# Two feed-forward layers with eight of 64 experts around a gated mixing layer, on one core: row transfers by index from POOL, and one product's halves issued together

## The chip, the cores and the metric

The kernel runs on one core of a Trainium2 chip. A core has five engines, each with its own queue of instructions in program order: PE (TensorE, matrix products and transposes), DVE (VectorE), ACT (ScalarE), POOL (GpSimd) and SP (SyncE, which here only issues transfers). Engines wait for each other through semaphores. The core's 16 DMA engines move data between the device memory and the on-chip memory. PE writes to PSUM, a small memory that DVE and ACT read.

The metric is the device time of one launch in microseconds (us). Lower is better.

## What is computed

The input `u` has 8 sequences of 512 tokens with 128 features, in float32. With x = u:

```python
x = x + 0.5 * ffn(layernorm(x))
x = x + mix(layernorm(x))
x = x + 0.5 * ffn(layernorm(x))          # the same weights again

def ffn(x):                              # 64 experts, hidden size 64, the best 8 per token
    shared = silu(x @ Ws_up) @ Ws_down
    aff = x @ centroids.T                # "logits"
    idx = top_k(aff + expert_biases, 8)
    w = sigmoid(aff[idx]);  w = w / (sum(w) + 1e-8)
    h = silu(einsum('td,edf->etf', x, W_up))
    y = einsum('etf,efd->etd', h, W_down)
    return shared + einsum('etd,te->td', y, cw)    # cw: w at the chosen experts, else 0

def mix(u):
    xf = u @ WB.T,  but the first token as it is
    xb = u @ WBf.T, but the last token as it is
    gamma = sigmoid(xf @ w1.T + xb @ w2.T + b)
    return gamma * (xf + xb) + (1 - gamma) * u
```

All 64 experts are computed for every token; those that were not chosen have weight 0.

## The kernel before

**Items.** The work is 16 items: `items` lists the two ffn layers, and within each the 8 sequences. An item is one sequence in one layer, held as four tiles of 128 tokens (`NT` = 4) in `xs[s]`, 128 partitions by 4 by 128. In the second layer `mix(s)` runs before the ffn of the sequence. Two experts make a pair (2 x 64 hidden = 128), so an item has 32 pairs (`NP`).

**The main loop** (L460 to L484) runs over n, 16 x 32 pairs and 25 more. It writes each engine's order out by hand, since `manual_schedule` keeps program order. Step n does this:

- `up(n)`: PE multiplies the pair's `W_up` with the item's transposed tokens `ut` into `ph` (128x512, L410). ACT writes silu of it to `h` (L412). Four `ph` buffers exist.
- `scale(n - 22)`: DVE multiplies `h` of 22 steps ago with the routing weights `cw` (L418). `load_cw` (L293) brings these from device memory on SP, four pairs at a time, broadcast over 64 partitions.
- `down(n - 25)`: PE multiplies the scaled `h` of 25 steps ago with `W_down` and accumulates into `y` (L428). After pair 31, ACT writes half of `y` to `yt` (L452).
- `finish(i)`, two steps after an item's last `down`: PE transposes `yt` four times into `po` (L396), DVE adds it to `xs[s]` (L397), and in the second layer SP issues one store of the sequence (L399).
- one step of `prep(i + 1)`, the preparation of the next item.

A float32 product is two instructions on PE in the profile (hence x1024 for 512 products).

**Preparation.** `prep(i)` is a generator: each `yield` ends its part of one step. It starts at pair 1 of the item before (for item 1: at pair 14 of item 0, `FIRST`). In order:

- in the second layer all of `mix(s)`: `stats`, `normed`, `turned`, the products `pfb`, the gate, the update of `xs[s]`
- `stats` (L179): DVE takes mean and variance of the four tiles (L184, L186), POOL makes `rstd` with an add and a power (L188, L189)
- `normed` (L192): four DVE instructions write `u` (L195)
- two yields later, `turned` (L205): four PE transposes into one PSUM buffer (L209), and ACT copies it to `ut` (L318)
- a step later the shared-and-logits product `sl` (L327): for each half of the tokens (256), one product with `wsl`, whose 128 columns are `Ws_up` and the transposed centroids. Half 0 has them in one order, half 1 in the other. DVE copies the logits' 64 rows to `lg` (L335), and ACT writes silu of the other 64 to `hsh` (L336)
- a step later PE transposes `lg` into `pa` (L342); then DVE and ACT choose the experts and make the weights; PE transposes these, and SP stores them to device memory (`cw_t`, L387, L388)

The loop that issues the two halves of `sl`, as it stands:

```python
for k in range(2):
    nc.tensor.matmul(sl[:, k, :], lhsT=wsl[:, k, :, :]..., rhs=ut[:, k * H : (k + 1) * H], ...)
    at, other = slice(k * F, (k + 1) * F), slice((1 - k) * F, (2 - k) * F)
    nc.vector.tensor_copy(lg[other, :], sl[other, k, :])
    nc.scalar.activation(hsh[at, :], sl[at, k, :], AF.Silu)
```

`sl` is one PSUM tile, `[P, 2, H]`.

**Transfers.** All are issued by SP, in program order. Ahead of the loop come sequence 0 (`load_x(0)`, L98), centroids, `Ws_up`, `W_up` in four parts, sequence 1 and half of `W_down`. `load_rest` (L137) is called at pair 14 of item 0, after the first four `load_cw`, and before the first step of `prep(1)`. It issues the rest: `Ws_down`, the other half of `W_down`, sequences 2 to 7, and the mixing layer's weights.

**Pools.** The PSUM pool `ps_m` has two buffers, shared by all transposes, `sl`, `pfb` and `po`. Each sequence has its own `xs` tile.

Of the kernel before, what the change touches and what calls it, by code (L numbers as in the profile page):

```python
# [8 lines left out]
F32 = mybir.dt.float32  # L9
AF = mybir.ActivationFunctionType  # L10
ALU = mybir.AluOpType
AX = mybir.AxisListType

P = 128
EPS_LN = 1e-5
# [11 lines left out]
def macaron_kernel(  # L27
# [34 lines left out]
    nc = tc.nc  # L62
    B, T, D = x.shape
    E, _, F = w_up.shape
    NT = T // P
# [3 lines left out]
    H = T // 2  # L69
    NH = NT // 2  # L70
    assert D == P and 2 * F == P and E == F and NT == 4 and NP % GROUP == 0

    const = ctx.enter_context(tc.tile_pool(name="const", bufs=1))
# [9 lines left out]
    ps_m = ctx.enter_context(tc.tile_pool(name="ps_m", bufs=2, space=bass.MemoryType.PSUM))  # L83
# [10 lines left out]
    warm = const.tile([P, 1], F32, name="warm")  # L94
    nc.scalar.activation(warm, ident[:, 0:1], AF.Silu)

    def load_x(s):
        nc.sync.dma_start(out=xs[s], in_=x[s].rearrange("(n p) d -> p n d", p=P))  # L98

    wup = const.tile([P, E, F], F32, name="wup")  # L100
    wdn = const.tile([P, NP, D], F32, name="wdn")
# [19 lines left out]
            in_=w_down[e0:e1].rearrange("(q two) f d -> (two f) q d", two=2),  # L121
        )

    load_x(0)
    nc.sync.dma_start(out=cent, in_=centroids)
    for k in range(2):
        nc.sync.dma_start(out=wsl[:, k, k, :], in_=ws_up)
# [9 lines left out]
    def load_rest():  # L137

        for k in range(2):
            nc.sync.dma_start(out=wsdn[k * F : (k + 1) * F, :], in_=ws_down)  # L140
        load_down(E // 2, E)
        for s in range(2, B):
            load_x(s)
        nc.sync.dma_start(out=wb_sb, in_=wb)
        nc.sync.dma_start(out=wbf_sb, in_=wbf)
        nc.sync.dma_start(out=w12[:, 0, :], in_=w1[0].partition_broadcast(P))
        nc.sync.dma_start(out=w12[:, 1, :], in_=w2[0].partition_broadcast(P))
        with nc.allow_non_contiguous_dma(reason="two columns, once"):
            nc.sync.dma_start(out=w12c[:, 0:1], in_=w1.rearrange("o d -> d o"))
            nc.sync.dma_start(out=w12c[:, 1:2], in_=w2.rearrange("o d -> d o"))  # L150
        nc.sync.dma_start(out=b_bc, in_=b.partition_broadcast(P))
# [24 lines left out]
        nc.scalar.mul(half_b, b_bc, 0.5)  # L176


    def stats(src, name):  # L179

        st = small.tile([P, NT, nc.vector.BN_STATS_DIM], F32, tag="st", name=f"st_{name}")
        mv = small.tile([P, NT, nc.vector.BN_AGGR_DIM], F32, tag="mv", name=f"mv_{name}")
        for j in range(NT):
            nc.vector.bn_stats(st[:, j, :], src[:, j, :])  # L184
        for j in range(NT):
            nc.vector.bn_aggr(mv[:, j, :], st[:, j, :])  # L186
        rstd = small.tile([P, NT], F32, tag="rstd", name=f"rstd_{name}")
        nc.gpsimd.tensor_scalar(rstd, mv[:, :, 1], EPS_LN, None, ALU.add)  # L188
        nc.gpsimd.tensor_tensor(rstd, rstd, minus_half, ALU.pow)  # L189
        return mv, rstd  # L190

    def normed(src, mv, rstd, width, name):  # L192
# [9 lines left out]
            )  # L202
        return u

    def turned(src, name):  # L205

        ps = ps_m.tile([P, 512], F32, tag="m", name=f"ps_{name}")
        for j in range(NT):
            nc.tensor.transpose(ps[:, j * P : (j + 1) * P], src[:, j, :D], ident)  # L209
        return ps  # L210

    def mix(s):
        xt = xs[s]
        mv, rstd = stats(xt, f"mix{s}")
        yield
        u = normed(xt, mv, rstd, D1, f"mix{s}")

        for k, j in ((0, 0), (1, NT - 1)):
            ew = norm.tile([P, D], F32, tag="ew", name=f"ew{s}_{k}")
            nc.vector.tensor_tensor(ew, u[:, j, :D], w12[:, k, :], ALU.mult)  # L220
            nc.vector.tensor_reduce(u[:, j, D:D1], ew, AX.X, ALU.add)
        yield
        yield
        ps = turned(u, f"mixt{s}")


        ut = norm.tile([P, T + 1], F32, tag="mixt", name=f"mixt{s}")
        nc.gpsimd.memset(ut[:, 0:1], 0.0)
        nc.gpsimd.memset(ut[:, T : T + 1], 0.0)
        nc.scalar.copy(ut[:, 1:T], ps[:, 1:T])  # L230
        yield
        yield
        gam = small.tile([P, NT], F32, tag="gam", name=f"gam{s}")
        halves = []
        for half in range(NT // 2):
            pfb = ps_m.tile([P, 2, D1], F32, tag="m", name=f"pfb{s}_{half}")
            halves.append(pfb)
            for k in range(2):
                j = 2 * half + k
                nc.tensor.matmul(  # L240
                    pfb[:, k, :],
                    lhsT=ut[:, j * P : (j + 1) * P],
                    rhs=mix_b,
                    start=True,
                    stop=False,
                )
                nc.tensor.matmul(  # L247
                    pfb[:, k, :],
                    lhsT=ut[:, j * P + 1 : (j + 1) * P + 1],
                    rhs=mix_bf,  # L250
                    start=False,
                    stop=True,
                )

            k, j, at = ((0, 0, 0), (1, NT - 1, P - 1))[half]
            nc.vector.scalar_tensor_tensor(  # L256
                pfb[:, k, :], u[:, j, :], ident[:, at : at + 1], pfb[:, k, :], ALU.mult, ALU.add
            )
            nc.scalar.activation(  # L259
                gam[:, 2 * half : 2 * half + 2],  # L260
                pfb[:, :, D],
                AF.Tanh,
                bias=half_b,
                scale=0.5,
            )
            yield
        sg = small.tile([P, NT], F32, tag="sg", name=f"sg{s}")
        nc.vector.tensor_scalar(sg, gam, 0.5, 0.5, ALU.mult, ALU.add)
        rest = small.tile([P, NT], F32, tag="rest", name=f"rest{s}")
        nc.vector.tensor_scalar(rest, gam, -0.5, 0.5, ALU.mult, ALU.add)  # L270
        for j in range(NT):
            nc.vector.scalar_tensor_tensor(
                xt[:, j, :],
                halves[j // 2][:, j % 2, :D],
                sg[:, j : j + 1],
                xt[:, j, :],
                ALU.mult,
                ALU.add,
            )
        yield  # L280
        for j in range(NT):
            nc.vector.scalar_tensor_tensor(
                xt[:, j, :], u[:, j, :D], rest[:, j : j + 1], xt[:, j, :], ALU.mult, ALU.add
            )
        yield
# [20 lines left out]
    def prep(i):  # L306

        layer, s = items[i]
        if layer == 1:
            yield from mix(s)  # L310
        mv, rstd = stats(xs[s], f"f{i}")
        yield
        u = normed(xs[s], mv, rstd, D, f"f{i}")
        yield
        yield
        ps = turned(u, f"ft{i}")
        ut = norm.tile([P, T], F32, tag="ut", name=f"ut{i}")
        nc.scalar.copy(ut, ps)  # L318
        uts[i] = ut
        yield  # L320

# [4 lines left out]
        for k in range(2):  # L326
            nc.tensor.matmul(  # L327
                sl[:, k, :],
                lhsT=wsl[:, k, :, :].rearrange("d a f -> d (a f)"),
                rhs=ut[:, k * H : (k + 1) * H],  # L330
                start=True,
                stop=True,
            )
            at, other = slice(k * F, (k + 1) * F), slice((1 - k) * F, (2 - k) * F)
            nc.vector.tensor_copy(lg[other, :], sl[other, k, :])  # L335
            nc.scalar.activation(hsh[at, :], sl[at, k, :], AF.Silu)  # L336
# [54 lines left out]
    def finish(i, yt):  # L391

        layer, s = items[i]
        po = ps_m.tile([P, NT, D], F32, tag="m", name=f"po{i}")
        for j in range(NT):
            nc.tensor.transpose(po[:, j, :], yt[:, j * P : (j + 1) * P], ident)  # L396
        nc.vector.tensor_tensor(xs[s], po, xs[s], ALU.add)  # L397
        if layer == 1:
            nc.sync.dma_start(out=out[s].rearrange("(n p) d -> p n d", p=P), in_=xs[s])  # L399


    hs = {}
# [21 lines left out]
    def down(n):  # L424
        i, pair = divmod(n, NP)
        if pair == 0 and i not in ys:
            ys[i] = ps_y.tile([P, T], F32, tag="y", name=f"y{i}")
        nc.tensor.matmul(  # L428
            ys[i],
            lhsT=wdn[:, pair, :],  # L430
            rhs=hs.pop(n),
            start=pair == 0 and i % 2 == 0,
            stop=pair == NP - 1,
        )


        if i % 2 == 0 and pair in SHARED:
            if i + 1 not in ys:
                ys[i + 1] = ps_y.tile([P, T], F32, tag="y", name=f"y{i + 1}")
            k = SHARED.index(pair)  # L440
            for at, item in sorted(((k, i), (1 - k, i + 1))):
                rows = slice(at * F, (at + 1) * F)
                nc.tensor.matmul(  # L443
                    ys[item][:, at * H : (at + 1) * H],
                    lhsT=wsdn[rows, :],
                    rhs=shared[item][rows, :],
                    start=item > i and k == 0,
                    stop=False,
                )
        if pair == NP - 1:  # L450
            yt = norm.tile([P, T], F32, tag="yt", name=f"yt{i}")
            nc.scalar.mul(yt, ys.pop(i), 0.5)  # L452
            later[n + 2] = lambda: finish(i, yt)

    total = len(items) * NP
# [71 lines left out]
```

## Time and profile before

| | |
|---|---|
| device time, median of 3 runs | 985.75 us (985.08 to 985.78) |
| the profiled execution: device time | 985.12 us |
| its span, first to last instruction | 983.0 us |
| granted TensorE clock, mean | 0.999 |
| `ph`, L410: 1024 instructions | 523.3 us busy, mean 595 ns |
| `y`, L428: 1024 instructions | 518.8 us busy, mean 592 ns |
| DVE `h` by `cw`, L418: 512 instructions | 322.1 us busy, mean 681 ns |
| ACT silu, L412: 512 instructions | 303.4 us busy, mean 597 ns |
| POOL `rstd`, L188 and L189 for the ffn: 16 each | 8.5 and 16.6 us busy |
| moved by SP's queue | 145.18 MB, 69.9% of the time of 16 DMA engines |

How to read the profile: a row of the groups gives line, engine, operation, output and inputs by their names in the program, shapes and count; behind the bar the busy time and the mean of one instruction in ns; behind the second bar how long the engine stood idle just before these instructions, and what ended most of that. A row of the timeline has start, duration, engine, line, operation, output and inputs, and in brackets the idle time before it with its releaser. PEld is the weight load of PE, which lies beside the products. SPq is SP's queue: its rows are the issuing of transfers, not the data on the way. Durations of PE overlap, since products are pipelined; the distance between two starts tells more.

### The profile page before, as it was taken

What the parts mean: (1) busy time and instruction counts of PE and PEld (TensorE: products, weight loads), DVE (VectorE), ACT (ScalarE), POOL (GpSimd) and SP (SyncE); (2) the same over time, 40 slices, a digit from 0 to 9 for tenths busy, and PEclk for the clock granted to TensorE, in tenths of its full rate; (3) what the DMA queues carried; (4) which work ended last, traced back from release to release, by engine and by line L of the source; (5) the groups of instructions that cost most, each with busy time, mean ns of one, the idle gap of its engine ahead of it and who ended that gap; (6) DMA issues with size and microseconds to landing.
All of it is one profiled execution on the core that took longest, in us unless ns stands there. A gap on an engine that the chain in (4) does not pass through costs nothing.

```text
span 983.0 us, 8249 instructions
## 1 busy us (share of the span) xinstructions
PE 954.5 (97%) x2535; PEld 440.8 (45%) x2535; DVE 476.2 (48%) x1280; ACT 398.8 (41%) x673; POOL 39.5 (4%) x71
## 2 busy tenths in 40 slices
PE   6999999999999999999999999999999999999998
PEld 3444444444444444444444444444444444444443
DVE  3444363524636154445464554645546456465242
ACT  4643343433434343334343343433435334343330
POOL 1000000000000000000000000000000000000000
PEclk9999999999999999999999999999999999999999
DMA  7999848686684868846678466783767837678933
GB/s 160 207 212 215 181 103 164 125 175 130 139 166 91 171 128 178 168 88 148 125 163 173 88 159 126 163 181 88 159 129 163 181 87 162 125 163 183 210 76 76
DMA packets 90156, 145.71 MB, mean 148 GB/s; under 512 B 10048, under 2 KB 24064, under 8 KB 90112
## 3 DMA queue, kind: packets, MB, share of 16 engines
q1 hardware_dynamic: 90112, 145.18, 69.9%
q8 instruction: 20, 0.33, 0.2%
q14 instruction: 24, 0.20, 0.1%
HBM read 140.97 MB, written 4.19 MB: 148 GB/s over the span
## 4 chain that ended last, share of the span: by engine, by line
PE 96%; ACT 1%; DVE 1%; DMA 0%; issue 0%; POOL 0%; ACTq 0%
PE y L428 45%; PE ph L410 44%; PE sl L327 2%; PE y L443 1%; PE ps_ft L209 1%; PE po L396 1%; PE pfb L247 1%; PE pfb L240 1%; DVE lg L335 1%; ACT hsh L336 1%; PE pa L342 0%; PE pc L379 0%; PE ps_mixt L209 0%; DMA x<-in_L_attn_u_dram 0%; ACT L412 0%
## 5 line engine op out<-in xcount | busy, mean ns | idle before, releaser
L410 PE MATMUL ph<-ut,wup 128*128 128x512 f32 x1024 | 523.3, 595 | 1.7 <-ACT h L412 1.7
L428 PE MATMUL y<-h,wdn 128*128 128x512 f32 x1024 | 518.8, 592 | 0.0
L412 ACT ACTIVATE h<-ph 128x512 f32<-128x512 f32 x512 | 303.4, 597 | 456.8 <-PE ph L410 429.4
L418 DVE TENSOR_TENSOR h<-h,cw 128x512 f32<-128x512 f32 x512 | 322.1, 681 | 54.7 <-DMA cw<-cw_t 50.7
L428 PEld LDWEIGHTS y<-h,wdn 128*128 128x128 f32 x1024 | 194.6, 190 | 244.9 <-issue 209.2
L410 PEld LDWEIGHTS ph<-ut,wup 128*128 128x128 f32 x1024 | 186.8, 191 | 196.3 <-issue 190.5
L397 DVE TENSOR_TENSOR x<-po,x 128x512 f32<-128x512 f32 x16 | 11.1, 692 | 192.8 <-PE po L396 192.8
L335 DVE COPY lg<-sl 64x256 f32<-64x256 f32 x32 | 13.5, 422 | 108.8 <-PE sl L327 108.8
L256 DVE SCALAR_TENSOR_TENSOR pfb<-u_mix,ident,pfb 128x129 f32<-128x129 f32 x16 | 5.7, 356 | 93.8 <-PE pfb L247 80.1
L327 PE MATMUL sl<-ut,wsl 128*128 128x256 f32 x64 | 22.0, 426 | 15.5 <-ACT hsh L336 14.9
L188 POOL TENSOR_SCALAR rstd_f<-mv_f 128x4 f32<-128x4 f32 x16 | 8.5, 532 | 516.8 <-DVE mv_f L186 516.8
L336 ACT ACTIVATE hsh<-sl 64x256 f32<-64x256 f32 x32 | 12.1, 378 | 38.7 <-DVE lg L335 38.7
L195 DVE TENSOR_SCALAR u_f<-x,mv_f,rstd_f 128x128 f32<-128x128 f32 x64 | 17.8, 342 | 20.4 <-POOL rstd_f L189 20.4
L327 PEld LDWEIGHTS sl<-ut,wsl 128*128 128x128 f32 x64 | 11.1, 196 | 30.0 <-ACT hsh L336 21.6
L353 ACT ACT_TABLE_LOAD x16 | 20.5, 1283 | 0.3
L412 ACT ACT_TABLE_LOAD x16 | 20.5, 1283 | 0.3
L452 ACT ACTIVATE yt<-y 128x512 f32<-128x512 f32 x16 | 9.6, 597 | 26.5 <-PE y L428 26.5
L184 DVE BATCH_NORM_STATS2 st_f<-x 128x6 f32<-128x128 f32 x64 | 13.8, 277 | 10.3 <-DMA x<-in_L_attn_u_dram 10.3
L188 POOL TENSOR_SCALAR rstd_mix<-mv_mix 128x4 f32<-128x4 f32 x8 | 4.6, 577 | 302.9 <-DVE mv_mix L186 302.9
L189 POOL TENSOR_TENSOR rstd_f<-rstd_f,minus_half 128x4 f32<-128x4 f32 x16 | 16.6, 1038 | 1.3
L318 ACT COPY ut<-ps_ft 128x512 f32<-128x512 f32 x16 | 9.4, 586 | 14.1 <-PE ps_ft L209 14.1
L259 ACT ACTIVATE gam<-pfb,half_b 128x2 f32<-128x2 f32 x16 | 4.2, 262 | 25.2 <-DVE pfb L256 25.2
(67 smaller groups left out, 282.1 us busy)
## 6 DMA issues: line engine op xcount, KB each, us to landing
cw<-cw_t SPq DMA_DIRECT2D x256, 512.0 KB, 7.1
x<-in_L_attn_u_dram SPq DMA_DIRECT2D x8, 256.0 KB, 5.7
cw_t<-cw_sb SPq DMA_DIRECT2D x32, 64.0 KB, 3.4
out_dram<-x SPq DMA_DIRECT2D x8, 256.0 KB, 2.3
wdn<-in_L_ffn_W_down_dram SPq DMA_DIRECT2D x2, 512.0 KB, 6.0
wup<-in_L_ffn_W_up_dram SPq DMA_DIRECT2D x2, 256.0 KB, 3.9
wup<-in_L_ffn_W_up_dram SPq DMA_DIRECT2D x1, 512.0 KB, 6.5
w<-in_L_attn_w_dram SPq DMA_DIRECT2D x2, 64.0 KB, 4.0
```

The lines of the kernel that those rows point to most:

```text
L184: nc.vector.bn_stats(st[:, j, :], src[:, j, :])
L188: nc.gpsimd.tensor_scalar(rstd, mv[:, :, 1], EPS_LN, None, ALU.add)
L189: nc.gpsimd.tensor_tensor(rstd, rstd, minus_half, ALU.pow)
L195: nc.vector.tensor_scalar(u[:, j, :D], src[:, j, :], mv[:, j, 0:1], rstd[:, j : j + 1], ALU.subtract, ALU.mult,)
L327: nc.tensor.matmul(sl[:, k, :], lhsT=wsl[:, k, :, :].rearrange("d a f -> d (a f)"), rhs=ut[:, k * H : (k + 1) * H], start=True, stop=True,)
L335: nc.vector.tensor_copy(lg[other, :], sl[other, k, :])
L336: nc.scalar.activation(hsh[at, :], sl[at, k, :], AF.Silu)
L353: nc.scalar.activation(sig, pa, AF.Sigmoid)
L410: nc.tensor.matmul(ph, lhsT=w, rhs=uts[i], start=True, stop=True)
L412: nc.scalar.activation(h, ph, AF.Silu)
L418: nc.vector.tensor_tensor(h, h, cw_tiles[group][:, g, :], ALU.mult)
L428: nc.tensor.matmul(ys[i], lhsT=wdn[:, pair, :], rhs=hs.pop(n), start=pair == 0 and i % 2 == 0, stop=pair == NP - 1,)
```

## The change

Five edits, in the order of the code:

- A tile `token` of row numbers, written once by POOL. Sequence 0 is loaded in two halves by SP. Sequences 2 to 7 are no longer loaded by SP: in `load_rest` POOL issues 24 indirect transfers, one for each tile of 128 tokens, with the row numbers from `token`.
- For item 0 alone, statistics, transposes and the copies to `ut` are made in two halves (`parts`). `turned` now takes the copy as a function.
- In `prep` the two products of `sl` are issued first, and the copies and activations of both halves follow.
- `finish` stores by POOL: four indirect transfers for each sequence, each naming all rows of `out` as its target and 128 row numbers. For the last item the transposes, the add and the stores are made in two halves.
- For the last item, ACT and DVE each write half of `yt`.

```diff
-    def load_x(s):
-        nc.sync.dma_start(out=xs[s], in_=x[s].rearrange("(n p) d -> p n d", p=P))
+    token = const.tile([P, B * NT], mybir.dt.int32, name="token")
+    nc.gpsimd.iota(token, [[P, B * NT]], base=0, channel_multiplier=1)
+
+    def rows_of(s, j):
+        n = s * NT + j
+        return bass.IndirectOffsetOnAxis(ap=token[:, n : n + 1], axis=0)
+
+    def load_x(s, a=0, e=NT):
+        src = x[s].rearrange("(n p) d -> p n d", p=P)
+        nc.sync.dma_start(out=xs[s][:, a:e, :], in_=src[:, a:e, :])
...
-    load_x(0)
+    load_x(0, 0, NH)
+    load_x(0, NH, NT)
...
         for s in range(2, B):
-            load_x(s)
+            for j in range(NT):
+                nc.gpsimd.indirect_dma_start(
+                    out=xs[s][:, j, :],
+                    out_offset=None,
+                    in_=x.rearrange("b t d -> (b t) d"),
+                    in_offset=rows_of(s, j),
+                )
...
-    def stats(src, name):
+    def stats(src, name, parts=1):
...
+        for part in range(parts):
+            js = range(part * NT // parts, (part + 1) * NT // parts)
+            for j in js:
+                nc.vector.bn_stats(st[:, j, :], src[:, j, :])
+            for j in js:
+                nc.vector.bn_aggr(mv[:, j, :], st[:, j, :])
+            at = slice(js[0], js[-1] + 1)
+            nc.gpsimd.tensor_scalar(rstd[:, at], mv[:, at, 1], EPS_LN, None, ALU.add)
+            nc.gpsimd.tensor_tensor(rstd[:, at], rstd[:, at], minus_half[:, at], ALU.pow)
...
-        ps = turned(u, f"ft{i}")
         ut = norm.tile([P, T], F32, tag="ut", name=f"ut{i}")
-        nc.scalar.copy(ut, ps)
+        turned(lambda a, e, ps: nc.scalar.copy(ut[:, a:e], ps), u, f"ft{i}", parts)
...
                 start=True,
                 stop=True,
             )
+        for k in range(2):
             at, other = slice(k * F, (k + 1) * F), slice((1 - k) * F, (2 - k) * F)
             nc.vector.tensor_copy(lg[other, :], sl[other, k, :])
             nc.scalar.activation(hsh[at, :], sl[at, k, :], AF.Silu)
...
-        po = ps_m.tile([P, NT, D], F32, tag="m", name=f"po{i}")
-        for j in range(NT):
-            nc.tensor.transpose(po[:, j, :], yt[:, j * P : (j + 1) * P], ident)
-        nc.vector.tensor_tensor(xs[s], po, xs[s], ALU.add)
-        if layer == 1:
-            nc.sync.dma_start(out=out[s].rearrange("(n p) d -> p n d", p=P), in_=xs[s])
+        parts = 2 if i == len(items) - 1 else 1
+        for part in range(parts):
+            js = range(part * NT // parts, (part + 1) * NT // parts)
+            po = ps_m.tile([P, len(js), D], F32, tag="m", name=f"po{i}_{part}")
+            for n, j in enumerate(js):
+                nc.tensor.transpose(po[:, n, :], yt[:, j * P : (j + 1) * P], ident)
+            at = slice(js[0], js[-1] + 1)
+            nc.vector.tensor_tensor(xs[s][:, at, :], po, xs[s][:, at, :], ALU.add)
+            if layer == 1:
+                for j in js:
+                    nc.gpsimd.indirect_dma_start(
+                        out=out.rearrange("b t d -> (b t) d"),
+                        out_offset=rows_of(s, j),
+                        in_=xs[s][:, j, :],
+                        in_offset=None,
+                    )
...
-            nc.scalar.mul(yt, ys.pop(i), 0.5)
+            y = ys.pop(i)
+            if i == len(items) - 1:
+                nc.scalar.mul(yt[:, :H], y[:, :H], 0.5)
+                nc.vector.tensor_scalar(yt[:, H:], y[:, H:], 0.5, None, ALU.mult)
+            else:
+                nc.scalar.mul(yt, y, 0.5)
```

## The prediction

> **What bounds the kernel now.** I read the page from the top: the busy shares, the chain that ended last, then the costliest groups. After that I asked for the timeline of three places that the change touches.
>
> ```profile
> PE 954.5 (97%) x2535; PEld 440.8 (45%) x2535; DVE 476.2 (48%) x1280; ACT 398.8 (41%) x673; POOL 39.5 (4%) x71
> ...
> PE 96%; ACT 1%; DVE 1%; DMA 0%; issue 0%; POOL 0%; ACTq 0%
> ...
> L327 PE MATMUL sl<-ut,wsl 128*128 128x256 f32 x64 | 22.0, 426 | 15.5 <-ACT hsh L336 14.9
> ```
>
> TensorE is the chain for 96% of the span. A gain must shorten what PE does or waits for, or lie before its first or after its last product; a loss must make PE wait. The third row is the only large PE wait: the second half of `sl` waits for ScalarE's read of the first, 14.9 us in 16 items. Its surroundings, in the timeline of a late item:
>
> ```profile
> 621.20 0.59 PE L327 MATMUL sl<-ut,wsl 128*128 128x256 f32 x2
> 621.84 0.43 DVE L335 COPY lg<-sl 64x256 f32<-64x256 f32 x1 [2.60 <-PE sl L327]
> 622.30 0.38 ACT L336 ACTIVATE hsh<-sl 64x256 f32<-64x256 f32 x1 [1.16 <-DVE lg L335]
> 622.73 0.70 PE L327 MATMUL sl<-ut,wsl 128*128 128x256 f32 x2 [0.93 <-ACT hsh L336]
> 623.26 1.02 PE L410 MATMUL ph<-ut,wup 128*128 128x512 f32 x2
> ```
>
> From the first half to the next product PE takes 623.26 - 621.20 = 2.06 us for two half products. A full product is 0.86 us (starts 625.20 and 626.06), a half 0.43.
>
> POOL does two short instructions per normalisation and no transfer. Its place in the second item's start, and the end of the kernel, from the timeline:
>
> ```profile
> 20.77 1.04 POOL L189 TENSOR_TENSOR rstd_f<-rstd_f,minus_half 128x4 f32<-128x4 f32 x1
> ...
> 30.10 0.60 PE L209 MATMUL ps_ft<-ident,u_f 128*128 128x128 f32 x4
> ...
> 977.55 0.60 ACT L452 ACTIVATE yt<-y 128x512 f32<-128x512 f32 x1 [21.78 <-PE y L428]
> ...
> 978.21 0.66 PE L396 MATMUL po<-ident,yt 128*128 128x128 f32 x4 [0.75 <-ACT yt L452]
> 978.90 0.69 DVE L397 TENSOR_TENSOR x<-po,x 128x512 f32<-128x512 f32 x1 [8.54 <-PE po L396]
> 979.62 0.38 SPq L399 DMA_DIRECT2D out_dram<-x  x1
> ```
>
> Here `rstd` of item 1 is ready at 21.8, and PE wants what hangs on it at 30.10: 8.3 us of slack. At the end one store issues at 979.62, and the span ends at 983.0.
>
> **What the Trainium skill says.** "DMA: Bandwidth & Descriptors", section "Specifications", gives about 1 us to the first byte for a transfer that POOL issues (Q7 cores write the descriptors) and 0.6 for one from SP. No POOL transfer is in this trace; SP's issues take 0.38 to 0.45 us. The same page, "Two DMAs through the same engine are not ordered", has the issuing engine wait on the completion semaphore where transfers depend on each other. That is what the instruction order of the changed program contains: every store of `out` waits for the store before it, since each names all 4096 rows as its target. "TensorE: Matmul & The Clock Gate", "Part 1: The HAM clock gate": after an idle window of about 3.4 us the array drops to half rate, for about as long. The trace agrees for the start: an `sl` half takes 1.01 us (10.77 to the next product at 11.78) against 0.43 later.
>
> **The change part by part.** Write T for the time that one indirect transfer of 128 rows holds POOL.
>
> *Back-to-back halves.* Items 2 to 15: 2.06 becomes 2 x 0.43 = 0.86, a gain of 1.20. The second `lg` copy now ends 0.43 + 0.64 + 0.43 + 0.03 + 0.38 + 0.03 + 0.42 = 2.36 after the first half's start (copy and activation still alternate). `pa`, which needs it, comes after one `ph` and one `y`, at 0.86 + 1.72 = 2.58, less about 0.2 for its weight load. So it nearly touches, and I take 1.15: 14 x 1.15 = 16.1. Item 1 has no `y` between: `sl` to `pa` was 31.43 to 34.45, 3.02, and becomes about 2.7: 0.3. Together **-16.4 us**.
>
> *Halved start of item 0.* Statistics, transposes and copies in halves, and no wait inside `sl`, start `ph` at about 9.4 instead of 11.78: at most **-2.4**, kept only if nothing waits later.
>
> *24 row loads on POOL.* They replace 6 loads on SP (15.22 us of its queue from 37.59, which PE never waited for, so nothing is gained there). In POOL's order they stand between `rstd` of item 0 and `rstd` of item 1. The queue behind them is `rstd`, then DVE's `u`, then PE's transposes at its 18th product. POOL is free at about 6.4 (1.28 us of `rstd` work twice, begun at 4.0 on the first half). Loads end at 6.4 + 24T, then 1.5 for `rstd`, then 1.45 for four normalisations (1.11) and the last transpose. The next `ph` starts then instead of at 30.54: **24T - 21.2** us. The 8.3 us of slack is paid at T = 0.88; below 0.79 the start's 2.4 us is kept.
>
> T is not in the trace. From below: a direct issue on SP, 0.45. From above: 2.15, the page's fit for a whole POOL transfer (section "Anatomy of one DMA — SWDGE (gpsimd) path": 2.0 + bytes/436e3), as if nothing overlapped. I take **T = 1.25**: the page's 1 us and a quarter, guessed, for fetching 128 row numbers. That gives +8.8. PE then idles over 3.4 us, so it restarts cold: about **+2.0** (half of the 4 us that the start shows). The 1.5 MB themselves are 6 us at the 246 GB/s of 13.5 to 16 us; weights have 10 us of room there, so nothing for that.
>
> *Stores in the middle.* Each takes T_s = T + 1.6 from issue to landing (SP's 256 KB store lands in 2.3 with 0.38 of issue, a 32 KB load in 2.0 with 0.52: between 1.5 and 1.9 after issue). Four in a row hold POOL 3 T_s + T = 9.8 us. After item 8 the residual add ends at 585.1, and PE wants `ps_mixt` at 601.37; `rstd`, `u` and the first transpose need about 3, so room for 13.5. **0**.
>
> *End.* Half `yt` on ACT beside half on DVE (0.4), two transposes (0.45) and a half add (0.4) let the first store issue at about 978.95, 0.65 sooner. Four stores, each after the one before, and 1.1 from landing to the end: 978.95 + 4 x 2.85 + 1.1 = 991.45, **+8.45**. The second half's work hides behind them.
>
> Sum: -16.4 + 8.8 + 2.0 + 8.45 = **+2.85**; in general 28T - 32.15, zero at T = 1.15. The profiled execution took 985.12 (span 983.0), which would become 988.0; the median of 985.75 is 0.63 above it, so 988.6. I say **988.5**.
>
> **Rivals.**
>
> *POOL is cheap (T at most 1.1): faster.* At T = 0.9: loads +0.4, no cold restart, end 978.95 + 4 x 2.5 + 1.1 - 983.0 = +7.05, halves -16.4, sum -8.95: 976.8. At 0.7, with the start kept: -16.4 - 2.4 + 6.25 = -12.55: 973.2. For it: the page's 1 us is latency and need not be all occupancy, and successive transfers may overlap. Against: POOL's power over four columns alone takes 1.04. It decides below T = 1.08.
>
> *POOL is dear (T about 2): much slower.* Then T_s is 3.6, with busy DMA queues (share 1.07 between 60 and 100 us) about 4.4 in the middle. 3 x 4.4 + 2 = 15.2 exceeds 13.5 in the five items whose stores precede another mix: 8.5. With 28 x 2 - 32.15 = 23.85: 1018. Against: that is nearly the page's whole transfer.
>
> *The halves give less than they seem.* If `lg` cannot read until late and PE waits for `pa` instead, half a microsecond per item returns, 7 us, and the forecast becomes 995.5. For it: the 0.2 us of room. Against: DVE was idle 2.60 us and ACT 1.16 before these reads.
>
> **How the numbers follow.** Less than 0.2%, 2 us, can't be told from no change. Forecast (T from 1.1 to 1.6): 0.43, its own range 984 to 999. Cheap POOL: 0.36. Dear POOL: 0.14. Weaker halves: 0.07. The range leaves out T under 0.85 and over about 1.7: 976 to 1005. Faster: 0.34 from cheap POOL and 0.01 from the rest. Same: T between 1.08 and 1.22, 0.15. Slower: 0.50.
>
> **What would show it.** Right: no PE wait at `sl` and steps of 0.86 there; a PE gap before `ps_ft` of item 1 of about 9 us, released through DVE by POOL; four stores in series at the end, about 2.9 us apart; the span's last PE product about 6 us earlier than before. Wrong: POOL's loads done before 27 us; stores that overlap; a PE wait at `pa`, or at `ps_mixt` after the stores.

## The result, and the profile after

The changed kernel takes 996.38 us (median of 4 runs, 995.42 to 998.32) against 985.49 us for the kernel before: ratio 1.0113, 95% interval 1.0096 to 1.0131. It is 10.9 us slower. The profiled execution took 998.32 us, the longest of the four, with a span of 996.5 us; the numbers of its profile are compared with the span before, 983.0 us. So the profile shows a loss of 13.5 us where the medians show 10.9; the other three executions have no profile.

From the page of the changed kernel, the busy shares, the chain, and three groups:

```profile
PE 957.0 (96%) x2535; PEld 443.0 (44%) x2535; DVE 475.6 (48%) x1282; ACT 398.9 (40%) x674; POOL 97.8 (10%) x130
...
PE 77%; issue 9%; DMA 6%; POOL 5%; DVE 2%; ACT 0%; POOLq 0%; ACTq 0%
...
L426 POOL DMA_INDIRECT out_dram<-x,token x32 | 35.8, 1119 | 311.9 <-DVE x L423 221.4
...
L154 POOL DMA_INDIRECT x<-in_L_attn_u_dram,token x24 | 23.5, 979 | 7.2 <-issue 7.2
...
L348 PE MATMUL sl<-ut,wsl 128*128 128x256 f32 x64 | 18.2, 411 | 0.0
```

The wait of 14.9 us at `sl` is gone, as its row shows. But PE's share of the chain fell from 96% to 77%: POOL, its transfers and unexplained time stand in the chain now. Four places of the timeline show where.

A late item's `sl`:

```profile
622.26 1.03 PE L348 MATMUL sl<-ut,wsl 128*128 128x256 f32 x4
623.12 1.02 PE L442 MATMUL ph<-ut,wup 128*128 128x512 f32 x2
...
624.19 0.42 DVE L357 COPY lg<-sl 64x256 f32<-64x256 f32 x1 [0.44 <-ACT hsh L358]
...
624.84 0.38 PE L364 MATMUL pa<-ident,lg 128*128 128x128 f32 x2
```

The next product starts 0.86 us after the first half (623.12 - 622.26), against 2.06 before. The second copy ends 2.35 after the first half's start, and `pa` starts at 2.58 without a wait.

The start of item 1, the last of the 24 loads and what comes behind them:

```profile
34.35 0.94 POOL L154 DMA_INDIRECT x<-in_L_attn_u_dram,token  x1 [0.30 <-issue]
35.60 0.94 POOL L154 DMA_INDIRECT x<-in_L_attn_u_dram,token  x1 [0.30 <-issue]
36.56 0.26 POOL L207 TENSOR_SCALAR rstd_f<-mv_f 128x4 f32<-128x4 f32 x1
36.90 1.05 POOL L208 TENSOR_TENSOR rstd_f<-rstd_f,minus_half 128x4 f32<-128x4 f32 x1
37.98 1.11 DVE L214 TENSOR_SCALAR u_f<-x,mv_f,rstd_f 128x128 f32<-128x128 f32 x4 [17.09 <-POOL rstd_f L208]
38.47 1.16 PE L230 MATMUL ps_ft<-ident,u_f 128*128 128x128 f32 x4 [11.90 <-DVE u_f L214]
39.42 1.92 PE L442 MATMUL ph<-ut,wup 128*128 128x512 f32 x2
```

A load is 0.94 us busy, but the next starts 1.25 us after it (a few of the early ones 1.3 to 1.6): 24 of them hold POOL from 6.0 to 36.5. The chain of releases is in the brackets: DVE waited 17.09 us for POOL, PE 11.90 us for DVE. The `sl` behind this product starts at 41.13, 1.71 us after it, twice the 0.86 of late items: PE restarted at half rate.

The middle, the stores of sequence 0 (item 8):

```profile
584.71 1.29 POOL L426 DMA_INDIRECT out_dram<-x,token  x1 [29.27 <-DVE x L423]
587.55 1.31 POOL L426 DMA_INDIRECT out_dram<-x,token  x1 [1.55 <-DMA out_dram<-x,token]
594.31 0.96 POOL L426 DMA_INDIRECT out_dram<-x,token  x1 [5.45 <-DMA out_dram<-x,token]
599.13 0.96 POOL L426 DMA_INDIRECT out_dram<-x,token  x1 [3.87 <-DMA out_dram<-x,token]
600.12 0.24 POOL L207 TENSOR_SCALAR rstd_mix<-mv_mix 128x4 f32<-128x4 f32 x1
...
601.52 1.11 DVE L214 TENSOR_SCALAR u_mix<-x,mv_mix,rstd_mix 128x128 f32<-128x128 f32 x4 [11.26 <-POOL rstd_mix L208]
602.02 1.01 PE L230 MATMUL ps_mixt<-ident,u_mix 128*128 128x128 f32 x4 [1.16 <-DVE u_mix L214]
```

Each store waits for the one before, and the gaps are uneven: 2.84, 6.76 and 4.82 us from start to start. POOL is held 15.4 us, and PE waits at `ps_mixt`, where it did not wait before (601.37 in the kernel before, with no wait listed).

The end, with the last row from the query on the program's closing line (how often; shortest, median and longest in ns; the starts of the first and the last):

```profile
982.15 0.96 POOL L426 DMA_INDIRECT out_dram<-x,token  x1 [10.82 <-DVE x L423]
984.66 0.96 POOL L426 DMA_INDIRECT out_dram<-x,token  x1 [1.55 <-DMA out_dram<-x,token]
987.64 0.96 POOL L426 DMA_INDIRECT out_dram<-x,token  x1 [2.03 <-DMA out_dram<-x,token]
990.14 0.96 POOL L426 DMA_INDIRECT out_dram<-x,token  x1 [1.55 <-DMA out_dram<-x,token]
```

```profile
L560 POOLq DRAIN  x3: 45/102/5837, 989.9 to 996.3; - x3
```

The last store is issued 8.0 us after the first. `DRAIN` is an instruction at the end of POOL's queue. The long one starts at 989.9, with the issue of the last store, and takes 5.84 us, up to 995.8; the program ends at 996.5.

PE's own starts, subtracted between the two timelines, place the 13.5 us of the profiled executions. Two rows of the kernel before that the table uses, and one after:

```profile
30.54 1.02 PE L410 MATMUL ph<-ut,wup 128*128 128x512 f32 x2
...
583.77 0.60 PE L396 MATMUL po<-ident,yt 128*128 128x128 f32 x4
```

```profile
583.09 0.60 PE L421 MATMUL po<-ident,yt 128*128 128x128 f32 x4
```

| reached on PE | after minus before, us | since the row above |
|---|---|---|
| last transposes of item 0's preparation, `pc` | -3.7 | halved start, and `sl` without its wait |
| first `ph` after `ps_ft` of item 1 (30.54; 39.42) | +8.9 | POOL's loads |
| `pc` of item 1 | +10.1 | cold restart, less 0.3 to 0.4 at `sl` |
| `po` of item 8 (583.77; 583.09) | -0.7 | nine times -1.20 at `sl` |
| `po` of item 13 | +3.0 | five times -1.20, so 9.6 lost at five `ps_mixt` |
| `po` of item 15 (978.21; 980.97) | +2.8 | the halved `yt` |
| end of the span | +13.5 | stores and drain: 10.7 |

Of the 9.6 us at `ps_mixt`, 5.1 are listed as waits, and 1.7 are a stretch at half rate after one of them (725.52, shown at the end). Most of the rest comes with every wait: the four transposes then follow each other 0.17 to 0.26 us apart, as DVE delivers `u_mix`, not at 0.11.

### The profile page after: what moved, and what is told of

Read it like the earlier page. It is cut to its first block, busy times and chain, and to the rows that moved or that the text cites. A ratio compares the mean times of both kernels' runs of the same rounds, so it can differ in the third digit from the quotient of the medians.

```text
span 996.5 us, 8326 instructions
## 1 busy us (share of the span) xinstructions
PE 957.0 (96%) x2535; PEld 443.0 (44%) x2535; DVE 475.6 (48%) x1282; ACT 398.9 (40%) x674; POOL 97.8 (10%) x130
## 4 chain that ended last, share of the span: by engine, by line
PE 77%; issue 9%; DMA 6%; POOL 5%; DVE 2%; ACT 0%; POOLq 0%; ACTq 0%
PE y L460 36%; PE ph L442 35%; DMA out_dram<-x,token 6%; POOL x L154 2%; PE sl L348 1%; POOL out_dram L426 1%; PE y L475 1%; PE ps_ft L230 1%; PE ps_mixt L230 1%; PE pfb L267 1%; PE pfb L260 1%; PE po L421 1%; POOL rstd_mix L208 1%; POOL rstd_f L208 0%; DVE h L450 0%
## 5 line engine op out<-in xcount | busy, mean ns | idle before, releaser
L423 DVE TENSOR_TENSOR x<-po,x 128x512 f32<-128x512 f32 (+1 forms) x17 | 11.2, 660 | 184.1 <-PE po L421 184.0
L426 POOL DMA_INDIRECT out_dram<-x,token x32 | 35.8, 1119 | 311.9 <-DVE x L423 221.4
L357 DVE COPY lg<-sl 64x256 f32<-64x256 f32 x32 | 13.5, 422 | 103.5 <-PE sl L348 96.4
L207 POOL TENSOR_SCALAR rstd_f<-mv_f 128x4 f32<-128x4 f32 (+1 forms) x17 | 8.7, 513 | 448.1 <-DVE mv_f L205 448.0
L214 DVE TENSOR_SCALAR u_mix<-x,mv_mix,rstd_mix 128x128 f32<-128x128 f32 x32 | 8.9, 343 | 61.0 <-POOL rstd_mix L208 61.0
L154 POOL DMA_INDIRECT x<-in_L_attn_u_dram,token x24 | 23.5, 979 | 7.2 <-issue 7.2
L230 PE MATMUL ps_ft<-ident,u_f 128*128 128x128 f32 x64 | 10.9, 294 | 13.1 <-DVE u_f L214 13.1
L339 ACT COPY ut<-ps_ft 128x512 f32<-128x512 f32 (+1 forms) x17 | 9.5, 561 | 24.8 <-PE ps_ft L230 24.8
L230 PEld LDWEIGHTS ps_ft<-ident,u_f 128*128 128x128 f32 x64 | 8.5, 146 | 21.9 <-issue 17.6
L348 PE MATMUL sl<-ut,wsl 128*128 128x256 f32 x64 | 18.2, 411 | 0.0
```

What stands on the lines that cost most here:

```text
L154: nc.gpsimd.indirect_dma_start(out=xs[s][:, j, :], out_offset=None, in_=x.rearrange("b t d -> (b t) d"), in_offset=rows_of(s, j),)
L214: nc.vector.tensor_scalar(u[:, j, :D], src[:, j, :], mv[:, j, 0:1], rstd[:, j : j + 1], ALU.subtract, ALU.mult,)
L230: nc.tensor.transpose(ps[:, n * P : (n + 1) * P], src[:, j, :D], ident)
L348: nc.tensor.matmul(sl[:, k, :], lhsT=wsl[:, k, :, :].rearrange("d a f -> d (a f)"), rhs=ut[:, k * H : (k + 1) * H], start=True, stop=True,)
L426: nc.gpsimd.indirect_dma_start(out=out.rearrange("b t d -> (b t) d"), out_offset=rows_of(s, j), in_=xs[s][:, j, :], in_offset=None,)
```

## The experiments

Each kernel ran beside the kernel before on the same chip. Ratios are to that, with the 95% interval. The median of the kernel before lay between 985.48 and 985.69 in all of them, so their times can be compared with each other too. "The place of PE" is its start at `po` of item 8 against the kernel before, as in the table above.

**The halves of `sl` alone**, in the kernel before:

```diff
                 start=True,
                 stop=True,
             )
+        for k in range(2):
             at, other = slice(k * F, (k + 1) * F), slice((1 - k) * F, (2 - k) * F)
             nc.vector.tensor_copy(lg[other, :], sl[other, k, :])
```

> The kernel before with the two products of sl issued back to back, and nothing else of the change. Theory (PE's wait for ScalarE's read is the whole cost): 1.19 us less in each of items 2 to 15 and about 1 us less in items 0 and 1 together, so 985.5 - 17.7 = about 968 us. Rival (the wait moves to pa, because lg now ends later): half a microsecond per item comes back, about 975 us, and PE shows waits at pa.

Measured: 966.71 us, ratio 0.981 (0.9794 to 0.9826), 18.9 us faster. The row of `sl` on its page:

```profile
L327 PE MATMUL sl<-ut,wsl 128*128 128x256 f32 x64 | 17.6, 399 | 0.7 <-ACT ut L318 0.7
```

No wait for `hsh` is left. PE gains 1.20 us in each of items 2 to 15, 1.26 in item 0 and 0.42 in item 1, where it waits 0.6 us at `pa`. The rival falls; this part is worth a little more than forecast.

**Loads back on SP**, the rest of the change kept:

```diff
         for s in range(2, B):
-            for j in range(NT):
-                nc.gpsimd.indirect_dma_start(out=xs[s][:, j, :], ..., in_offset=rows_of(s, j))
+            load_x(s)
```

> The changed kernel with sequences 2 to 7 loaded by SP as before. Theory (the 24 loads hold POOL ahead of rstd of item 1, and PE waits 12 us and restarts cold): PE stands 3.7 us ahead of the kernel before at the start and keeps that, instead of being 10.1 behind: 996.4 - 14 = about 982.5 us, no wait at ps_ft of item 1. Rival (the loads cost little and the start is late for another reason): 994 or more.

Measured: 980.64 us, ratio 0.9955 (0.9938 to 0.9972), 15.7 us less than the changed kernel. The place of PE is -14.7 instead of -0.7. The wait at `ps_ft` of item 1 is gone.

**POOL held by other work**, loads on SP, to tell POOL's time from the early traffic:

```diff
+        hold = const.tile([P, NT], F32, name="hold")
+        nc.gpsimd.memset(hold, 2.0)
+        for _ in range(28):
+            nc.gpsimd.tensor_tensor(hold, hold, minus_half, ALU.pow)
         for s in range(2, B):
             load_x(s)
```

> As the run with the loads on SP, but POOL runs 28 powers on a scratch tile (about 1.05 us each, 30 us) where the loads stood; the results of these powers are not used. Theory (it is POOL's time alone that delays rstd of item 1): the wait of about 12 us at ps_ft of item 1 is back, about 996 us. Rival (the early traffic of the row loads delays sequence 1 and the weights): no early traffic here, so about 982.5 us.

Measured: 992.17 us, ratio 1.0067 (1.005 to 1.0084). POOL's timeline, and PE's at the same place:

```profile
5.93 31.14 POOL L155 TENSOR_TENSOR hold<-hold,minus_half 128x4 f32<-128x4 f32 x28
37.04 0.23 POOL L205 TENSOR_SCALAR rstd_f<-mv_f 128x4 f32<-128x4 f32 x1
```

```profile
38.91 1.15 PE L228 MATMUL ps_ft<-ident,u_f 128*128 128x128 f32 x4 [12.40 <-DVE u_f L212]
39.86 1.91 PE L440 MATMUL ph<-ut,wup 128*128 128x512 f32 x2
```

Without a single row load, PE waits 12.40 us, and its place is -0.2, as in the changed kernel. So it is POOL's time in front of `rstd`, not the traffic. That the total is 4 us under 996 lies behind this place. What is lost at `ps_mixt` differs between runs, 5.7 us here and 9.6 in the changed kernel's profile, and the end, from the last `po` on, is 2.0 us shorter (13.6 against 15.6): POOL drains for 3.88 us instead of 5.84, although it issued the same last stores.

**The same 24 loads, later.** `load_tokens` holds the 24 indirect loads, taken out of `load_rest`; POOL issues them after `rstd` of item 1:

```diff
         mv, rstd = stats(xs[s], f"f{i}", parts)
+        if i == 1:
+            load_tokens()
```

> The changed kernel with the same 24 row loads on POOL, issued after rstd of item 1 instead of before it. Theory (their place in POOL's order is the cost, not the transfers): as with the loads on SP, about 981 us, with no wait at ps_ft of item 1; POOL is then busy from 21 to 51 us, and rstd of item 2 is wanted after that. Rival (the wait moves to item 2, whose tokens and rstd now come late): 985 or more, with a PE wait at ps_ft of item 2.

Measured: 983.69 us (10 runs, 981.63 to 985.65), ratio 0.9982 (0.9972 to 0.9991). PE's place is -14.9, as with the loads on SP, and nothing waits at item 2. So their place in the order was what PE paid for. The 3 us above the run with SP's loads come after item 8. In the two profiles, 5.4 us apart, it is 3.6 at `ps_mixt` (11.2 us lost here, 7.6 there) and 2.0 at the end, where the drain takes 5.84 us here and 3.88 there.

**Stores back on SP**, loads on POOL:

```diff
-                for j in js:
-                    nc.gpsimd.indirect_dma_start(out=..., out_offset=rows_of(s, j), in_=xs[s][:, j, :], ...)
+                nc.sync.dma_start(
+                    out=out[s].rearrange("(n p) d -> p n d", p=P)[:, at, :], in_=xs[s][:, at, :])
```

> The changed kernel with all results stored by SP (the last sequence in two halves), loads still by POOL. Theory (the stores cost at the end, where each waits for the one before, and in the middle, where they hold POOL ahead of rstd_mix): the end gives back about 10.5 us and the five waits at ps_mixt 7 to 9: about 978 us. Rival (the middle stores cost nothing, as the prediction had it, and the PE displacement there has another cause): about 986 us, with PE waits at ps_mixt still there.

Measured: 977.23 us, ratio 0.9916 (0.99 to 0.9933), 19.2 us less than the changed kernel. No wait at `ps_mixt` is left. The span ends 4.2 us after the start of the last `po` (15.5 in the changed kernel).

**Only the last sequence on SP:**

```diff
             if layer == 1:
+                if i == len(items) - 1:
+                    nc.sync.dma_start(out=out[s]...[:, at, :], in_=xs[s][:, at, :])
+                    continue
```

> The changed kernel with only the last sequence stored by SP, in two halves; the other seven still by POOL. Theory (four chained stores and POOL's own draining at the end make the tail): about 10 us less, 986.5 us, and the span ends about 4 us after the residual add, as in the kernel before. Rival (POOL drains long at the end even when its transfers landed before): 3 us of it stay, about 989.5 us.

Measured: 985.76 us (12 runs), ratio 1.0004 (0.9995 to 1.0013), 10.6 us less than the changed kernel. The waits at `ps_mixt` are still there (4.5 us listed), the tail from the last `po` on is 5.1 us. POOL's long drain happens here too, but it starts 15.7 us before the end, and nothing waits for it:

```profile
L566 POOLq DRAIN  x3: 45/102/5512, 967.2 to 982.6; - x3
```

**Stores on POOL, direct**, each to its own rows, so that none names another's target:

```diff
                 for j in js:
-                    nc.gpsimd.indirect_dma_start(out=..., out_offset=rows_of(s, j), in_=xs[s][:, j, :], ...)
+                    nc.gpsimd.dma_start(out=out[s, j * P : (j + 1) * P, :], in_=xs[s][:, j, :])
```

> The changed kernel with its stores still on POOL, but as direct transfers of 128 rows to their own rows of out, so that none waits for the one before. Theory (the chain of waits is what makes the stores dear): four issues in a row at about 1.25 us each, POOL free after 5 us instead of 15, no PE wait at ps_mixt (7 to 9 us less), and the last store is issued 4 us sooner: about 984.5 us. Rival (POOL transfers land late whatever they wait for, beside SP's traffic): 993 or more.

Measured: 981.26 us, ratio 0.9957 (0.994 to 0.9974), 15.1 us less. POOL's timeline after item 8:

```profile
584.64 2.29 POOL L426 DMA_DIRECT2D out_dram<-x  x4 [29.27 <-DVE x L423]
589.72 0.57 POOL L207 TENSOR_SCALAR rstd_mix<-mv_mix 128x4 f32<-128x4 f32 x1 [2.78 <-DVE mv_mix L205]
```

Four stores take 2.29 us, not the 5 that I expected: without row numbers an issue is about 0.57 us. POOL waits for DVE again, and no wait at `ps_mixt` is left. This run takes away both the chain and the row numbers. But four unchained stores at 1.25 us, 5 us in all, would also fit into the room of about 13.5 us before `ps_mixt`. So, by this sum, the chain is the cost in the middle, not POOL as the issuer; an unchained indirect store was not run.

**A quarter of SP's traffic.** The changed kernel, with `load_cw` and the multiplication using the weights of the first 128 tokens for all four tiles; the weights of the other 384 tokens are left out:

```diff
-        rows = cw_ts[i][2 * GROUP * q : 2 * GROUP * (q + 1), :].rearrange(
+        rows = cw_ts[i][2 * GROUP * q : 2 * GROUP * (q + 1), :P].rearrange(
...
-        nc.vector.tensor_tensor(h, h, cw_tiles[group][:, g, :], ALU.mult)
+        h3 = h.rearrange("p (n t) -> p n t", t=P)
+        w = cw_tiles[group][:, g, :].unsqueeze(1).to_broadcast([P, NT, P])
+        nc.vector.tensor_tensor(h3, h3, w, ALU.mult)
```

> The changed kernel, but load_cw brings the weights of the first 128 tokens only, and DVE uses them for all four tiles of a sequence: a quarter of SP's bytes; the weights of the other 384 tokens are left out. Theory (the stores in the middle land late because they queue beside SP's bursts of cw): the chained stores follow each other every 2.5 to 3 us there as at the end, POOL is free after about 9 us, no PE wait at ps_mixt, 7 to 10 us less: about 988 us. Rival (they land late whatever else is moved): 994 or more, with the waits at ps_mixt.

Measured: 988.54 us, ratio 1.003 (1.0019 to 1.0042). The chained stores of item 8:

```profile
583.91 1.29 POOL L426 DMA_INDIRECT out_dram<-x,token  x1 [29.27 <-DVE x L423]
586.74 1.32 POOL L426 DMA_INDIRECT out_dram<-x,token  x1 [1.54 <-DMA out_dram<-x,token]
590.12 0.96 POOL L426 DMA_INDIRECT out_dram<-x,token  x1 [2.06 <-DMA out_dram<-x,token]
592.61 0.95 POOL L426 DMA_INDIRECT out_dram<-x,token  x1 [1.54 <-DMA out_dram<-x,token]
```

They now take 8.7 us from the first start to the last, not 14.4. In the five sequences whose stores stand before another mix it is 8.6 to 10.6 us, not 14.4 to 15.0, and PE waits nowhere at `ps_mixt`. So the long gaps that PE pays for come from the traffic of `cw` beside them; which part of the way is crowded, the DMA engines or the memory, was not told apart. In the seventh sequence, where PE does not wait for them, one gap of 11.7 us remains, and its cause is open.

**All on SP**, with the halves at `sl`, start and end: the edits of the second and the fifth experiment together, without `token`.

> The changed kernel with all loads and stores of tokens on SP, keeping the back-to-back halves and the halved start and end. Theory (the halves at start and end are worth 2.3 us and 0.6 us, nothing else remains): the run with the halves only (966.7) less 2.9: about 964 us. Rival (the costs of loads and stores simply add): 996.4 - 15.7 - 19.2 = 961.5 us.

Measured: 963.24 us, ratio 0.9777 (0.9761 to 0.9793). This is 2.2% less than the kernel before. Its page has `PE` at 99% of a span of 961.2 us. The costs do not quite add: 15.7 and 19.2 us would leave 961.5. About 2 us are counted twice. The drain is 2.0 us longer with the 24 loads than without them; the run with SP's loads saves these 2.0, and so does the one with SP's stores, where the drain is over long before the end. What the stores cost in the middle also depends on the run.

**All on POOL, direct:** the same 24 loads and 32 stores as direct transfers.

> The changed kernel with all its POOL transfers, 24 loads and 32 stores, as direct transfers of the same 128 rows: same engine, same count, same bytes, no row numbers and no shared target. Theory (a direct transfer holds POOL for about 0.53 us as in the run with direct stores, an indirect one for 1.25): the loads end at 6 + 24 x 0.53 = 19 us, before rstd of item 1 is due, so no wait at ps_ft; no wait at ps_mixt; what is left over the run with everything on SP is POOL's draining at the end, about 3 us: 966 to 967 us. Rival (24 transfers on POOL before rstd cost much in any form): 978 or more.

Measured: 968.29 us, ratio 0.9826 (0.981 to 0.9843). POOL's timeline:

```profile
5.63 4.51 POOL L147 DMA_DIRECT2D x<-in_L_attn_u_dram  x8
13.08 4.29 POOL L147 DMA_DIRECT2D x<-in_L_attn_u_dram  x8 [2.94 <-DMA x<-in_L_attn_u_dram]
19.63 4.30 POOL L147 DMA_DIRECT2D x<-in_L_attn_u_dram  x8 [2.26 <-DMA x<-in_L_attn_u_dram]
23.96 0.24 POOL L195 TENSOR_SCALAR rstd_f<-mv_f 128x4 f32<-128x4 f32 x1
```

Eight loads go out at 0.54 us each, then POOL waits until an older one has landed. They end at 23.9, later than the 19 I expected, but still early enough: `ps_ft` of item 1 does not wait. Over the run with all on SP 5.1 us remain: 0.5 before `pc` of item 1, and 4.5 at the end, where POOL drains for 5.40 us; about 3 were expected there.

## Why the prediction was right or wrong

The direction, slower, was right, and 996.4 lies in the range of 976 to 1005. The size was not: +2.85 was forecast, +10.9 measured. Being right on the direction was partly luck: T was guessed, the sum turns at T = 1.15, and the two terms below that failed both failed on the slower side. Step by step, against the profiled execution:

- *Halves of `sl`, -16.4:* measured -1.20 in each of 14 items (-16.7) and -0.4 in item 1. The fear of a wait at `pa` came true only in item 1.
- *Halved start, at most -2.4:* PE stood 3.7 us ahead at `pc` of item 0. It was lost to the loads, as the step said; kept, it shows in the runs with the loads on SP.
- *24 loads, +8.8 at T = 1.25:* T, the quantity that was not in any trace, is 1.25 (start to start), and the next `ph` came 8.88 later. The value itself was a guess inside wide bounds, so that it was met is luck. The sum around it held: all 24 took 30.5 us instead of 30.0, but began 0.4 sooner. The run with POOL held by powers shows the mechanism.
- *Cold restart, +2.0:* about 1.6 (10.1 - 8.9, and the 0.4 that `sl` gained meanwhile).
- *Stores in the middle, 0:* this term failed. The prediction took 2.85 us per store, as beside idle queues, and held POOL for 9.8 us; room was 13.5. Beside SP's `cw` bursts the stores took 2.84, 6.76 and 4.82, POOL was held 15.4, and the five waits cost 9.6 us in the profile, a half-rate stretch of 1.7 included. The rival "POOL is dear" had this mechanism, the room of 13.5 us and nearly the size (8.5), but tied it to T = 2. The quarter-traffic run shows that a crowded queue was enough at T = 1.25.
- *End, +8.45:* measured +10.5 (10.7 less the 0.2 that the halved `yt` gained). The chain was as forecast, with 2.51, 2.98 and 2.50 from store to store against 2.85. What was not in the sum is POOL's drain. It starts with the last issue and takes 5.84 us, up to 995.8; the landing of the last store, after which the sum had 1.1 us left to the end, is about 3 us sooner (2.6 from issue, by the page's median, so 992.7).

So what was missing is one term set to zero (9.6 us in the profile) and one term without the drain (2.1 us), less about 1 us by which the other terms came out better. The cheap-POOL rival was wrong in T for indirect transfers, and right for direct ones: with T at 0.54 to 0.57 and no chain between the stores the kernel is faster than before.

Of the signs that were named for "right", three came: no wait at `sl`, a gap before `ps_ft` of item 1 that POOL ends through DVE (11.9 us, about 9 forecast), and four stores in series at the end. The fourth did not: PE's last products were to start 6 us earlier than before and started 2.8 later. Of the signs for "wrong", the wait at `ps_mixt` after the stores came.

## What to carry to other kernels

Before transfers move to an engine that also does small work for others, count its time per issue, and put them behind the work that someone waits for: the same 24 loads cost PE 14 us before `rstd` of item 1 and nothing at that place after it. Look for waits between transfers that name the same target; a chain pays the landing of each, and here the steps of a chain were up to 7.2 us long beside a busy queue where PE waited for them, and 2.5 to 3.0 alone at the end. Where POOL issues the last transfer of the program, count its drain, too: it took 3.9 us with 32 transfers in the program and 5.8 with 56. Price each part by itself: here a gain of 19 us in one line was hidden, since the rest of the change cost 30 in sum.

## What the runs showed of the hardware that was not expected

- An indirect transfer of 128 rows holds POOL for 1.25 us from start to start, a direct one of the same rows for about 0.54. The Trainium skill ("DMA: Bandwidth & Descriptors", section "Specifications") gives about 1 us for transfers that POOL issues and does not tell the two kinds apart. That figure is the latency to the first byte, not the time for which POOL is held, so it could not have given T.
- POOL's drain at the program's end was longer the more transfers POOL had issued in the whole program, however long ago. The run with SP's loads ends with the same four stores as the changed kernel, yet POOL drains there for 3.88 us instead of 5.84:

```profile
L554 POOLq DRAIN  x3: 45/102/3880, 973.9 to 978.3; - x3
```

  | POOL's transfers | runs | longest drain, us | of it after POOL's last instruction |
  |---|---|---|---|
  | none | before; halves alone; all on SP | 1.13 to 1.15 | 0.06 |
  | 24 loads | stores on SP | 3.13 | 2.05 |
  | 32 stores | loads on SP; POOL held | 3.88 | 2.69 |
  | 24 loads, 28 stores | only the last sequence on SP | 5.51 | 4.33 |
  | 24 loads, 32 stores | changed; loads later; quarter of the traffic | 5.84 | 4.65 |
  | 24 loads, 32 direct stores | stores direct; all direct | 5.41; 5.40 | 4.65 |

  The last column grows by about 0.082 us for each transfer of 64 KB, direct or indirect. Their number and their bytes were not varied apart, and why it is so is open.
- PE fell to half rate after a wait of only 1.71 us. In the timeline of the changed kernel the next three products start 1.63 and 1.71 us apart instead of 0.86:

```profile
725.52 1.01 PE L230 MATMUL ps_mixt<-ident,u_mix 128*128 128x128 f32 x4 [1.71 <-DVE u_mix L214]
...
726.36 1.83 PE L442 MATMUL ph<-ut,wup 128*128 128x512 f32 x2
...
727.99 1.91 PE L460 MATMUL y<-h,wdn 128*128 128x512 f32 x2
...
729.70 0.67 PE L442 MATMUL ph<-ut,wup 128*128 128x512 f32 x1
```

  "TensorE: Matmul & The Clock Gate", section "Part 1: The HAM clock gate", has an idle window of about 3.4 us for that; here a wait of half that length sufficed, in one of the five waits of this profile. The length alone does not decide: a wait of 1.99 us in the run with the later loads was followed by half rate, but one of 1.84 us in the same run and one of 1.72 us in the run with SP's loads were not. The traces suggest what does. Two rows of the profile's table of stretches (start and end, length, busy time of each engine, granted clock) show the clock, `PEclk`, halved for one stretch of 3.41 us, behind one in which PE is idle for 1.71 of 3.41 us:

```profile
core 0: us, PE busy (x) PEld busy (x) DVE busy (x) ACT busy (x) POOL busy (x), PEclk, DMA share, GB/s
723.03:726.44 3.41, 1.70 (x7) 0.66 (x6) 1.38 (x6) 0.56 (x1) 1.94 (x5) 1.00 0.06 19
726.44:729.86 3.42, 3.42 (x6) 1.36 (x6) 3.11 (x7) 1.18 (x2) 0.00 (x0) 0.50 0.00 0
```

  Within each trace of this case all changes of the granted clock lie whole multiples of 3.413 us apart. Cut into these stretches, the waits of 1.71 and 1.99 us each lie inside one of them, while those of 1.84 and 1.72 us are split, with at most 1.30 and 0.93 us in one. Of the stretches at full rate, none with 1.38 us of idle time or less was followed by half rate, and all with 1.71 us or more were (none lies between). This is read from the traces; no run moved a wait to test it.
